# Three of seven skip products moved into the states' accumulation, and an instruction planner that chooses by replays

## The chip, the cores and the metric

The kernel runs on one core of one Trainium2 chip. The metric is the device time of one launch in microseconds (us), median of three runs. The engines are named as in the profile: PE is TensorE's matmul side and PEld its weight loads, DVE is VectorE, ACT is ScalarE, POOL is GpSimd, SP is the engine that issues nearly all DMAs.

## The reference

Four residual layers on x of shape (4, 1024, 256), all in float32. Layer 1 is causal attention, layers 2 and 4 are the same channel mix, layer 3 is a state-space layer. The change lies in layer 3.

```python
xn = layernorm(x) * ln_g + ln_b
x_proj, z = split(xn @ W_in.T + b_in)              # 256 columns each
z = silu(z)
B_proj = x_proj @ W_B.T * dt.mean()                # 16 states
x_mean = causal_conv(B_proj, A_mean)               # along the tokens, per state
y = (x_mean @ W_C.T + D_skip * x_proj) * z
x = x + y @ W_out.T + b_out

# layers 2 and 4 (the mix)
r = sigmoid(xr @ W_r.T); k = relu(xk @ W_k.T) ** 2 # xr, xk: x mixed with the token before
x = x + r * (k @ W_v.T)
```

## The kernel before

**Tiling.** Each of the four batches b is two halves j = 2b and 2b + 1 of 512 tokens. A half is kept once by rows (128 tokens x 256 features, four times) and once turned, as columns: two blocks c of 128 features x 512 tokens. A product of one 128 x 128 weight block with 512 columns is the unit of work here. Two PSUM pools hold products: four single banks ("bank") and two double banks ("pair").

**Seven products instead of eight.** For a batch the 2 x 2 weight blocks meet a 2 x 2 arrangement of data (two feature blocks, two halves). `seven_products` (L821) makes the four results with seven products rather than eight, in the manner of Strassen and Winograd: `weight_sums` gives four sums of weight blocks, `stream_sums` (L796) gives four sums T1 to T4 of data blocks, on POOL or DVE. Each product p1 to p7 goes to a bank of its own, and VectorE adds it to what is there. This is used for the attention's queries (tiles p_qs), for the gates z (p_zs), for the skip D_skip * x_proj (p_ss, written to the tiles skip) and for the last mix's keys (p_gks).

**The states' share.** The convolution gives x_mean; SP writes it to memory (m_dram) and reads it back turned (xmT), per batch with four DMAs each way (`states_in`, L1829). For batch 0 `skip(0)` and `skip(1)` make the skip by plain products into a pair, and `mix_states` (L1920) adds x_mean @ W_C.T in the same banks. For batches 1 to 3 `skips_of_batch` (L1866) makes the skip with seven products, and `mix_states_apart` (L1880) makes x_mean @ W_C.T into the two pairs, as four matmuls of 16 rows that lie in four different row groups of TensorE. Then `grown` (L1899) adds these to the skip on VectorE, and `gated` (L1903) multiplies by z on POOL or DVE. `state_outputs` multiplies by W_out (tiles pr_pyo), and x is grown by the result (L1956).

**Order by hand, order by plan.** The order of TensorE's work is written out by hand in the kernel's main part. Gates and skips of batches 1 to 3 form one stream, `all_gates`, and `more_gates(n)` takes n products from it between other units, to cover the time in which those wait. The orders of the other engines come from `Order`: all work is logged with estimated costs and needs, `_due` (backwards) gives each operation the time by which TensorE needs it, and `_run` plays the program forwards on a model and takes, engine by engine, what is due first. `finish` (L178) tries 20 plans (share, margin, wait) in five rounds each; after a round, `_hurry` brings forward the dues of what TensorE waited for. The plan and dues with the earliest modelled end are then played once more, and this time the instructions are emitted. The same plan rules the whole program.

Of the kernel before, what the change touches and what calls it, by code (L numbers as in the profile page):

```python
# [4 lines left out]

# [39 lines left out]
def columns(n, k=1):  # L45

    return 2 * k * max(n * 0.845e-3, 0.105)
# [5 lines left out]
class Order:  # L53
# [23 lines left out]
        for share, margin in ((0.2, 2.5), (0.1, 1.5), (0.3, 4.0), (0.2, 1.5), (0.1, 2.5))  # L77
        for wait in (0.0, 0.08, 0.15, 0.22)
    ]
    ROUNDS = 5  # L80
    TRIALS = 4
    BANKS = {"bank": 4, "pair": 2}
# [95 lines left out]
    def finish(self):  # L178
        dues = self._due()
        self.made = {e["key"]: n for n, e in enumerate(self.log) if e["key"] is not None}  # L180
        self.ends = []
        best = math.inf
        for plan in self.PLANS:
            self.due = list(dues)
            for k in range(self.ROUNDS):
                used = list(self.due)
                end = self._run(plan, False)
                self.ends.append((end, k, plan))
                if end < best:
                    best, chosen = end, (plan, used)  # L190
                for key, wait in self.waits:
                    self._hurry(key, wait)
        plan, self.due = chosen
        self._run(plan, True)

    def _hurry(self, key, wait):

# [8 lines left out]
    def _run(self, plan, emits):  # L206
        self.SHARE, self.MARGIN, self.WAIT = plan
        self.emits = emits
        self.waits = []
        self.now = self.at = 0.0  # L210
        self.free, self.ready, self.offered = {}, {}, []
        self.queue = self.port = 0.0
        self.waiting = {}
        self.psum = {kind: [0.0] * k for kind, k in self.BANKS.items()}
        for n, e in enumerate(self.log):
            if e["kind"] == "op":
                self._enter(n)
            elif e["kind"] == "known":
                self._done(e["key"], e["time"])
            elif e["kind"] == "take":  # L220
                heapq.heappop(self.psum[e["takes"]])
            else:
                self._unit(e)
        while self.offered:
            self._step()
        return max(self.now, *self.free.values())
# [57 lines left out]
    def _step(self):  # L284
        self.at, k = self._first()
        time, n = self.offered.pop(k)
        e = self.log[n]
        end, _, engine, emit = self._way(time, n)
        engine, _, port = engine.partition("+")
        self.free[engine] = end  # L290
        if port or engine == "POOL":
            self.port = end
        if self.emits:
            emit()
        if e["frees"]:
            heapq.heappush(self.psum[e["frees"]], end + self.LAG)
        if e["moves"]:
            for k, work in enumerate(e["moves"]):
                issued = end - (len(e["moves"]) - 1 - k) * self.log[n]["cost"] / len(e["moves"])
                self.queue = max(self.queue, issued + self.FLIGHT) + work  # L300
            self._done(e["key"], self.queue + self.LANDING)
        else:
            self._done(e["key"], end + e["lag"])
# [46 lines left out]
def hybrid_kernel(  # L350
# [470 lines left out]
    def seven_products(key, sums_key, a, s_of, src, t_of, out, bias, needs, there):  # L821


        u = lazy(lambda: slot(f"u_{key}")[:, :HALF])

        def unit(r, w, data, need):
            p = lazy(lambda: bank(f"p{r}_{key}"))
            o.unit(
                f"{key}.p{r}", columns(HALF), needs + need,
                lambda: nc.tensor.matmul(p(), lhsT=w(), rhs=data(), start=True, stop=True), "bank",  # L830
            )
            return p

        def add(name, r, p, more, dst, e, need, last=True):

            def emit():
                if e is None or bias is None:
                    nc.vector.tensor_add(dst(), p(), more())
                else:
                    nc.vector.scalar_tensor_tensor(  # L840
                        dst(), p(), bias(e), more(), ALU.add, ALU.add
                    )
            o.op(
                f"{key}.{name}", [f"{key}.p{r}"] + [f"{key}.{k}" for k in need],
                ("DVE", dve(HALF) + 0.03, emit), frees="bank" if last else None,
            )

        def block(e, h):
            return lambda: out(e, h)

        p = unit(1, lambda: a(0, 0), lambda: src(0)[:, 0, :], there)
        o.op(f"{key}.u1", [f"{key}.p1"], *copies(u, p), frees="bank")
        yield
        p = unit(2, lambda: a(0, 1), lambda: src(0)[:, 1, :], there)
# [12 lines left out]
        add("c22", 5, p, u, block(1, 1), 1, ["u3"], last=False)  # L867
        add("v12", 5, p, block(0, 1), block(0, 1), 0, ["u3"])
        yield
        p = unit(3, lambda: s_of(4), lambda: src(1)[:, 1, :], there)  # L870
        add("c12", 3, p, block(0, 1), block(0, 1), None, ["v12"])
        yield
# [993 lines left out]
    def skips_of_batch(b):  # L1866

        there = columns_of(2 * b) + columns_of(2 * b + 1)
        src = lambda h, xb=(xnT[2 * b], xnT[2 * b + 1]): xb[h]()
        for j in (2 * b, 2 * b + 1):  # L1870
            skips[j] = lazy(lambda j=j: cols(f"skip_{j}"))
        sb = [skips[2 * b], skips[2 * b + 1]]
        sums_of_batch(b + 1)
        yield from seven_products(
            f"ss{b}", f"zs{b}", wx_block, lambda k: x_sums[:, k - 1, :], src, sums_of_batch(b),
            lambda e, h: sb[h]()[:, e, :], lambda e: b_skip[:, e : e + 1],
            ["x_sums", "b_all"], there,
        )

    def mix_states_apart(b):  # L1880

        for h in range(2):
            py[2 * b + h] = lazy(lambda h=h: pair(f"py_{2 * b + h}"))

        def emit():
            for e in range(KC):
                for h in range(2):
                    k = 2 * e + h
                    nc.tensor.matmul(
                        py[2 * b + h]()[:, ts(e, HALF)],  # L1890
                        lhsT=w_c[k * GRP : k * GRP + S, ts(e, P)],
                        rhs=xmT[b]()[k * GRP : k * GRP + S, ts(h, HALF)],
                        start=True,
                        stop=True,
                    )

        def grown(j, e):
            t = skips[j]()[:, e, :]
            nc.vector.tensor_add(t, py[j]()[:, ts(e, HALF)], t)  # L1899

        def gated(engine, j, e):
            t = z[j]()[:, e, :]
            engine.tensor_mul(t, t, skips[j]()[:, e, :])  # L1903

        o.unit(f"pm{b}", 1.0, ["w_c", f"xmT{b}"], emit, "pair", many=2)
        for h in range(2):
            j = 2 * b + h
            for e in range(KC):
                o.op(
                    f"g{e}.{j}", [f"pm{b}", f"ss{b}.c{e + 1}{h + 1}"],  # L1910
                    ("DVE", dve(HALF) + 0.03, partial(grown, j, e)),
                    frees="pair" if e else None,
                )
                o.op(
                    f"y{e}.{j}", [f"g{e}.{j}", f"z{e}.{j}"],
                    ("POOL", 1.05, partial(gated, nc.gpsimd, j, e)),
                    ("DVE+port", dve(HALF), partial(gated, nc.vector, j, e)),
                )
# [208 lines left out]
    for b in range(NB):  # L2127
        states_in(b)
    skip(1)
    more_gates(8)  # L2130
    mix_states(0)
    more_gates(8)
    outputs(0)
    more_gates(5)
    mix_states_apart(1)
    outputs(1)
    more_gates(4)
    outputs(2)
    more_gates(4)
    mix_states_apart(2)  # L2140
    outputs(3)
    more_gates(3)
# [86 lines left out]
```

## Time and profile before

| what | us |
|---|---|
| median of 3 runs | 465.42 (465.42 to 465.47) |
| profiled execution | 465.0 |
| its span, first to last instruction | 463.1 |
| PE busy in the span | 456.0 |
| DVE busy | 390.2 |
| ACT busy | 220.8 |
| POOL busy | 143.1 |

The profile is of one execution, so a sum made from it is made against its own 465.0 and its span of 463.1. The median of the runs shown is 0.4 above that execution. The program's stages follow each other in the span roughly so: loads and first scores to 20; attention with the first mix between its rows to 287; the states' convolution to 310; skips, gates and outputs of the state layer to 385, the last mix's first halves among them; the rest of the last mix to the end. Matmuls overlap a little in the records, so their cost is better read from start to start than from the listed duration.

### The profile page before, as it was taken

What the parts mean: (1) busy time and instruction counts of PE and PEld (TensorE: products, weight loads), DVE (VectorE), ACT (ScalarE), POOL (GpSimd) and SP (SyncE); (2) the same over time, 40 slices, a digit from 0 to 9 for tenths busy, and PEclk for the clock granted to TensorE, in tenths of its full rate; (3) what the DMA queues carried; (4) which work ended last, traced back from release to release, by engine and by line L of the source; (5) the groups of instructions that cost most, each with busy time, mean ns of one, the idle gap of its engine ahead of it and who ended that gap; (6) DMA issues with size and microseconds to landing.
All of it is one profiled execution on the core that took longest, in us unless ns stands there. A gap on an engine that the chain in (4) does not pass through costs nothing.

```text
span 463.1 us, 6634 instructions
## 1 busy us (share of the span) xinstructions
PE 456.0 (98%) x2052; PEld 312.5 (67%) x2052; DVE 390.2 (84%) x931; ACT 220.8 (48%) x463; POOL 143.1 (31%) x149
## 2 busy tenths in 40 slices
PE   8999999999999999999999999999999999999996
PEld 5766785667786667786777775474565758675875
DVE  3687769899969999889999977459889999999962
ACT  3422414454342433333556567441458777664652
POOL 3000102112013213121271354962052616826340
PEclk9999999999999999999999999999999999999999
DMA  8047876848455763427866989603022024252442
GB/s 242 21 127 203 250 190 168 222 132 258 117 135 139 221 194 93 118 62 237 224 177 182 275 268 271 260 17 88 11 92 91 1 86 144 81 147 99 129 144 84
DMA packets 84915, 69.44 MB, mean 150 GB/s; under 512 B 20160, under 2 KB 82576, under 8 KB 84880
## 3 DMA queue, kind: packets, MB, share of 16 engines
q1 hardware_dynamic: 84064, 68.76, 50.8%
q10 hardware_dynamic: 816, 0.26, 0.2%
q8 instruction: 16, 0.26, 0.2%
q14 instruction: 19, 0.16, 0.1%
HBM read 40.54 MB, written 28.45 MB: 149 GB/s over the span
## 4 chain that ended last, share of the span: by engine, by line
PE 86%; DVE 8%; issue 2%; DMA 1%; POOL 1%; ACT 1%; SPq 0%; DVEq 0%; POOLq 0%
PE po L1597 13%; PE sc L1492 13%; PE pv L1464 5%; PE p_zs L830 4%; PE p_ss L830 4%; PE p_qs L830 2%; PE p_gks L830 2%; PE py L1848 2%; PE pc L1798 2%; PE dust L1282 1%; DMA blocks_a<-rows_a 1%; PE pr_g0.pr L881 1%; PE pb L1735 1%; PE pp_a0.pq L774 1%; PE pr_g0.pv L881 1%
## 5 line engine op out<-in xcount | busy, mean ns | idle before, releaser
L1597 PE MATMUL po<-v,prT 128*128 128x256 f32 x288 | 67.7, 380 | 0.1
L1492 PE MATMUL sc<-xa,q 128*128 128x512 f32 (+3 forms) x192 | 67.0, 486 | 0.0
L1597 PEld LDWEIGHTS po<-v,prT 128*128 128x128 f32 x288 | 54.2, 189 | 11.6 <-issue 2.6
L1513 ACT ACTIVATE pr<-pr,nmx 128x128 f32<-128x128 f32 (+7 forms) x32 | 24.7, 773 | 64.6 <-DVE pr L1508 57.7
L1492 PEld LDWEIGHTS sc<-xa,q 128*128 128x128 f32 x192 | 35.1, 190 | 24.5 <-issue 19.6
L1464 PE MATMUL pv<-wv,xa 128*128 128x257 f32 x128 | 32.9, 380 | 0.0
L642 POOL TENSOR_TENSOR rs_a<-ve_a,minus_half 128x4 f32<-128x4 f32 x7 | 7.1, 1010 | 76.8 <-DVE ve_a L629 76.8
L1044 POOL TENSOR_TENSOR x<-x,r_f 128x512 f32<-128x512 f32 x16 | 20.3, 1271 | 33.0 <-DVE r_f L1038 32.5
L642 POOL TENSOR_TENSOR rs_h<-ve_h,minus_half 128x8 f32<-128x8 f32 x8 | 13.2, 1647 | 52.5 <-DVE ve_h L631 52.5
L1464 PEld LDWEIGHTS pv<-wv,xa 128*128 128x128 f32 x128 | 23.6, 191 | 7.8 <-issue 3.6
L1508 DVE TENSOR_SCALAR_CACHE_REDUCE pr<-sc,v 128x128 f32<-128x128 f32 (+7 forms) x32 | 26.2, 818 | 1.1
L1550 DVE STREAM_TRANSPOSE prT<-pblocks 128x384 f32<-128x384 f32 (+7 forms) x30 | 23.8, 793 | 2.4 <-DMA pblocks<-exps 2.3
L642 POOL TENSOR_TENSOR rs_f<-ve_f,minus_half 128x4 f32<-128x4 f32 x8 | 8.4, 1053 | 47.1 <-DVE ve_f L629 28.8
L1044 POOL TENSOR_TENSOR x<-x,r_g 128x512 f32<-128x512 f32 x14 | 18.9, 1371 | 11.0 <-DVE r_g L1038 11.0
L1641 POOL TENSOR_TENSOR x<-x,bout_r 128x512 f32<-128x512 f32 x16 | 20.0, 1279 | 4.5 <-ACT x L1634 4.5
L1606 DVE SCALAR_TENSOR_TENSOR x<-po,rsm,x 128x256 f32<-128x256 f32 x32 | 15.0, 470 | 4.3 <-PE po L1597 3.8
L1474 DVE TENSOR_TENSOR v<-pv,bv_r 128x257 f32<-128x257 f32 x32 | 13.4, 418 | 5.6 <-PE pv L1464 5.6
L930 DVE SCALAR_TENSOR_TENSOR xr_g<-hT_g,mur,xr_g 128x512 f32<-128x512 f32 x16 | 17.3, 1112 | 0.0
L663 ACT ACTIVATE xn_f<-x,mrs_f,rs_f 128x256 f32<-128x256 f32 x18 | 9.8, 592 | 15.5 <-DVE mrs_f L651 15.5
L1634 ACT ACTIVATE x<-x,mrs_h,rs 128x256 f32<-128x256 f32 x32 | 16.9, 592 | 0.0
L1903 POOL TENSOR_TENSOR z<-z,skip 128x512 f32<-128x512 f32 x9 | 13.1, 1462 | 10.9 <-DVE skip L1899 10.7
L663 ACT ACTIVATE xn_g<-x,mrs_g,rs_g 128x256 f32<-128x256 f32 x23 | 12.4, 589 | 8.3 <-DVE mrs_g L626 6.7
(458 smaller groups left out, 1089.8 us busy)
## 6 DMA issues: line engine op xcount, KB each, us to landing
hk<-r_dram SPq DMA_DIRECT2D x16, 512.0 KB, 9.2
rows_g<-xn_g SPq DMA_DIRECT2D x8, 512.0 KB, 2.9
blocks_g<-rows_g SPq DMA_DIRECT2D x32, 128.0 KB, 2.8
x<-in_L_attn_a_X_dram SPq DMA_DIRECT2D x7, 512.0 KB, 4.9
rows_f<-xn_f SPq DMA_DIRECT2D x7, 512.0 KB, 3.0
blocks_f<-rows_f SPq DMA_DIRECT2D x28, 128.0 KB, 2.7
rows_h<-xn_h SPq DMA_DIRECT2D x7, 512.0 KB, 3.7
blocks_h<-rows_h SPq DMA_DIRECT2D x28, 128.0 KB, 3.2
```

Of the source, the lines that this page charges most:

```text
L642: nc.gpsimd.tensor_tensor(rs()[:, :k].rearrange("p k n -> p (k n)"), ve()[:, :k].rearrange("p k n -> p (k n)"), minus_half[:, : k * NH], A ...
L663: nc.scalar.activation(place(n), split(row(n)), AF.Identity, bias=mrs()[:, k - 1, n : n + 1], scale=rs()[:, k - 1, n : n + 1],)
L830: lambda: nc.tensor.matmul(p(), lhsT=w(), rhs=data(), start=True, stop=True), "bank",
L930: nc.vector.scalar_tensor_tensor(t()[:, c, :], hT()[:, c, :HALF], mu1[:, c : c + 1], t()[:, c, :], ALU.mult, ALU.add,)
L1044: nc.gpsimd.tensor_add(xg, xg, r()[:, ts(g, 2), :])
L1464: nc.tensor.matmul(pv()[:, : D + 1], lhsT=xaj()[:, c, ts(n, P)], rhs=wv[:, c, :], start=(c == 0), stop=(c == KC - 1),)
L1492: nc.tensor.matmul(sc()[:, k * HALF : k * HALF + w], lhsT=qh()[:, c, ts(n, P)], rhs=keys[k]()[:, c, :w], start=(c == 0), stop=(c == KC - 1),)
L1508: nc.vector.tensor_scalar(dst, src, v[2 * b + h]()[:, n, D : D + 1], None, ALU.add, ALU.min, accum_out=nmx(),)
L1513: nc.scalar.activation(p()[:, :nk], p()[:, :nk], AF.Exp, bias=nmx(), scale=-1.0, accum_out=sm())
L1550: nc.vector.transpose(dst()[:, : NH * width].rearrange("p (k m a) -> p k m a", m=NH, a=GRP), blocks().rearrange("p m (k a) -> p k m a", a= ...
L1597: nc.tensor.matmul(po()[:, :D], lhsT=src()[:, ts(n, P)], rhs=v[2 * b + n // NH]()[:, n % NH, :D], start=(n == 0), stop=(n == t),)
L1641: nc.gpsimd.tensor_add(xg, xg, bout_r.unsqueeze(1).to_broadcast([P, 2, D]))
```

## The change

It has two parts.

First, the skips. The products p2, p4 and p3 of the seven each go into one result only, and nothing else is made from them. After the change they are no longer evicted on their own. `skips_of_batch` makes only p1, p6, p7 and p5 and keeps the partial sums u1, u4, u3, u5 in the four blocks of the skip tiles. `mix_states_apart` makes the other three with start=True and stop=False in the pairs' banks and lets the 16-row matmuls of the states accumulate onto them; the fourth bank, k == 3, is opened by the states' matmul itself. `grown` adds the bias b_skip along with the partial sum. The stream `all_gates` becomes nine turns shorter, and the numbers of `more_gates` are changed with it.

Second, the choice of a plan. After each modelled run, `_replays` plays the order that it gave six times more, with costs stretched at random (DVE up to 3%, ACT 4%, POOL 25%) and landings of transfers up to 0.6 us late, the seeds being fixed. The mean end of these replays, not the end of the run, is what plans are compared by, and the waits that occur in them are what `_hurry` is given.

```diff
@@ class Order @@
+    SAMPLES = 6
+    SPREAD = {"DVE": 0.03, "ACT": 0.04, "POOL": 0.25}
+    LATE = 0.6
@@ finish @@
                 used = list(self.due)
-                end = self._run(plan, False)
+                self._run(plan, False)
+                end = self._replays()
...
+    def _replays(self):
+        lost, ends = {}, 0.0
+        for k in range(self.SAMPLES):
+            rng = random.Random(k)
+            ends += self._replay(rng, lost)
+        self.waits = [(key, t / self.SAMPLES) for key, t in lost.items() if t > 0.1 * self.SAMPLES]
+        return ends / self.SAMPLES
...
+    def _replay(self, rng, lost):
+        for n, way in self.trail:
...
+            at = max(at, free.get(engine, 0.0), port if shared or engine == "POOL" else 0.0)
+            spread = self.SPREAD.get(engine, 0.0)
+            at += cost * (1.0 + spread * rng.random())
...
+                at = queue + self.LANDING + self.LATE * rng.random()
@@ skips_of_batch @@
-        yield from seven_products(
-            f"ss{b}", f"zs{b}", wx_block, lambda k: x_sums[:, k - 1, :], src, sums_of_batch(b),
-            lambda e, h: sb[h]()[:, e, :], lambda e: b_skip[:, e : e + 1],
-            ["x_sums", "b_all"], there,
-        )
+        u1, u2, u3, u5 = block(0, 0), block(0, 1), block(1, 0), block(1, 1)
+        p = unit(1, lambda: wx_block(0, 0), lambda: xnT[2 * b]()[:, 0, :], there)
+        o.op(f"{key}.u1", [f"{key}.p1"], *copies(u1, p), frees="bank")
+        yield
+        p = unit(6, lambda: x_sums[:, 1, :], lambda: T(2), [f"zs{b}.T2"])
+        add("u2", 6, p, u1, u2, "u1")
+        yield
+        p = unit(7, lambda: x_sums[:, 2, :], lambda: T(3), [f"zs{b}.T3"])
+        add("u3", 7, p, u2, u3, "u2")
+        yield
+        p = unit(5, lambda: x_sums[:, 0, :], lambda: T(1), [f"zs{b}.T1"])
+        add("u5", 5, p, u3, u5, "u3", last=False)
+        add("u4", 5, p, u2, u2, "u3")
+        yield
@@ mix_states_apart @@
         def emit():
+            for h, e, w, data in (
+                (0, 0, wx_block(0, 1), xnT[2 * b]()[:, 1, :]),
+                (0, 1, wx_block(1, 1), T(4)),
+                (1, 0, x_sums[:, 3, :], xnT[2 * b + 1]()[:, 1, :]),
+            ):
+                nc.tensor.matmul(
+                    py[2 * b + h]()[:, ts(e, HALF)], lhsT=w, rhs=data, start=True, stop=False
+                )
...
-                        start=True,
+                        start=(k == 3),
...
-            nc.vector.tensor_add(t, py[j]()[:, ts(e, HALF)], t)
+            nc.vector.scalar_tensor_tensor(
+                t, py[j]()[:, ts(e, HALF)], b_skip[:, e : e + 1], t, ALU.add, ALU.add
+            )
...
-        o.unit(f"pm{b}", 1.0, ["w_c", f"xmT{b}"], emit, "pair", many=2)
+        o.unit(
+            f"pm{b}", columns(HALF, 3) + 1.05,
+            ["w_c", "x_sums", "b_all", f"xmT{b}", f"zs{b}.T4"] + there, emit, "pair", many=2,
+        )
@@ main part @@
     skip(1)
-    more_gates(8)
+    more_gates(6)
     mix_states(0)
-    more_gates(8)
+    more_gates(5)
     outputs(0)
-    more_gates(5)
+    more_gates(3)
     mix_states_apart(1)
     outputs(1)
-    more_gates(4)
+    more_gates(3)
     outputs(2)
-    more_gates(4)
+    more_gates(3)
     mix_states_apart(2)
```

More of the change, by code (lines that the diff above doesn't have):

```diff
@@ L2 @@
 import math
+import random
 from contextlib import ExitStack
@@ L194, in finish @@
         self._run(plan, True)
+    def _replays(self):
[6 more added lines that the diff above has]
+    def _replay(self, rng, lost):
+        now = queue = port = 0.0
+        free, ready = {}, {}
+        psum = {kind: [0.0] * k for kind, k in self.BANKS.items()}
+        for n, way in self.trail:
+            e = self.log[n]
+            if e["kind"] == "known":
+                ready[e["key"]] = e["time"]
+                continue
+            if e["kind"] == "take":
+                heapq.heappop(psum[e["takes"]])
+                continue
+            last, at = None, 0.0
+            for k in e["needs"]:
+                if ready[k] > at:
+                    last, at = k, ready[k]
+            if e["kind"] == "unit":
+                for _ in range(e["many"] if e["takes"] else 0):
+                    at = max(at, heapq.heappop(psum[e["takes"]]))
+                if last is not None and at > now + 0.1:
+                    lost[last] = lost.get(last, 0.0) + at - now
+                now = max(now, at) + e["cost"]
+                ready[e["key"]] = now + self.LAG
+                continue
+            engine, shared, cost = way
+            if e["moves"]:
+                at = max(at, queue - self.FLIGHT - 0.5)
+            at = max(at, free.get(engine, 0.0), port if shared or engine == "POOL" else 0.0)
+            spread = self.SPREAD.get(engine, 0.0)
+            at += cost * (1.0 + spread * rng.random())
+            free[engine] = at
+            if shared or engine == "POOL":
+                port = at
+            if e["frees"]:
+                heapq.heappush(psum[e["frees"]], at + self.LAG)
+            if e["moves"]:
+                for k, work in enumerate(e["moves"]):
+                    issued = at - (len(e["moves"]) - 1 - k) * e["cost"] / len(e["moves"])
+                    queue = max(queue, issued + self.FLIGHT) + work
+                at = queue + self.LANDING + self.LATE * rng.random()
+            else:
+                at += e["lag"]
+            if e["key"] is not None:
+                ready[e["key"]] = at
+        return max(now, *free.values())
     def _hurry(self, key, wait):
@@ L208, in _run @@
         self.emits = emits
-        self.waits = []
+        self.waits, self.trail = [], []
         self.now = self.at = 0.0
@@ L218, in _run @@
             elif e["kind"] == "known":
+                self.trail.append((n, None))
                 self._done(e["key"], e["time"])
             elif e["kind"] == "take":
+                self.trail.append((n, None))
                 heapq.heappop(self.psum[e["takes"]])
@@ L223, in _run @@
                 self._unit(e)
+                self.trail.append((n, None))
         while self.offered:
@@ L287, in _step @@
         e = self.log[n]
-        end, _, engine, emit = self._way(time, n)
+        end, start, engine, emit = self._way(time, n)
         engine, _, port = engine.partition("+")
+        self.trail.append((n, (engine, port, end - start)))
         self.free[engine] = end
@@ L1868, in skips_of_batch, with block, unit, add @@
         there = columns_of(2 * b) + columns_of(2 * b + 1)
-        src = lambda h, xb=(xnT[2 * b], xnT[2 * b + 1]): xb[h]()
+        key = f"ss{b}"
+        T = sums_of_batch(b)
         for j in (2 * b, 2 * b + 1):
             skips[j] = lazy(lambda j=j: cols(f"skip_{j}"))
-        sb = [skips[2 * b], skips[2 * b + 1]]
         sums_of_batch(b + 1)
-        yield from seven_products(
-            f"ss{b}", f"zs{b}", wx_block, lambda k: x_sums[:, k - 1, :], src, sums_of_batch(b),
-            lambda e, h: sb[h]()[:, e, :], lambda e: b_skip[:, e : e + 1],
-            ["x_sums", "b_all"], there,
-        )
+        def block(e, h):
+            return lambda: skips[2 * b + h]()[:, e, :]
+        def unit(r, w, data, need):
+            p = lazy(lambda: bank(f"p{r}_{key}"))
+            o.unit(
+                f"{key}.p{r}", columns(HALF), ["x_sums", "b_all"] + need,
+                lambda: nc.tensor.matmul(p(), lhsT=w(), rhs=data(), start=True, stop=True), "bank",
+            )
+            return p
+        def add(name, r, p, more, to, need, last=True):
+            o.op(
+                f"{key}.{name}", [f"{key}.p{r}", f"{key}.{need}"],
+                ("DVE", dve(HALF) + 0.03, lambda: nc.vector.tensor_add(to(), p(), more())),
+                frees="bank" if last else None,
+            )
[13 more added lines that the diff above has]
+        yield
     def mix_states_apart(b):
@@ L1883, in mix_states_apart @@
             py[2 * b + h] = lazy(lambda h=h: pair(f"py_{2 * b + h}"))
+        T = sums_of_batch(b)
         def emit():
+            for h, e, w, data in (
[6 more added lines that the diff above has]
+                )
             for e in range(KC):
@@ L1898, in grown @@
             t = skips[j]()[:, e, :]
-            nc.vector.tensor_add(t, py[j]()[:, ts(e, HALF)], t)
+            nc.vector.scalar_tensor_tensor(
+                t, py[j]()[:, ts(e, HALF)], b_skip[:, e : e + 1], t, ALU.add, ALU.add
+            )
         def gated(engine, j, e):
@@ L1903, in gated @@
             engine.tensor_mul(t, t, skips[j]()[:, e, :])
-        o.unit(f"pm{b}", 1.0, ["w_c", f"xmT{b}"], emit, "pair", many=2)
+        there = columns_of(2 * b) + columns_of(2 * b + 1)
+        o.unit(
+            f"pm{b}", columns(HALF, 3) + 1.05,
+            ["w_c", "x_sums", "b_all", f"xmT{b}", f"zs{b}.T4"] + there, emit, "pair", many=2,
+        )
         for h in range(2):
@@ L1909, in mix_states_apart @@
                 o.op(
-                    f"g{e}.{j}", [f"pm{b}", f"ss{b}.c{e + 1}{h + 1}"],
+                    f"g{e}.{j}", [f"pm{b}", f"ss{b}." + (("u1", "u4"), ("u3", "u5"))[e][h]]
+                    + ([f"ss{b}.u2"] if (e, h) == (0, 0) else [])
+                    + ([f"ss{b}.u5"] if (e, h) == (1, 0) else []),
                     ("DVE", dve(HALF) + 0.03, partial(grown, j, e)),
```

## The prediction

> **What bounds the kernel now.** First the page's head and busy rows, then the busy times by stage.
>
> ```profile
> span 463.1 us, 6634 instructions
> PE 456.0 (98%) x2052; PEld 312.5 (67%) x2052; DVE 390.2 (84%) x931; ACT 220.8 (48%) x463; POOL 143.1 (31%) x149
> ```
>
> ```profile
> core 0: us, PE busy (x) PEld busy (x) DVE busy (x) ACT busy (x) POOL busy (x), PEclk, DMA share, GB/s
> 0.00:20.00 20.00, 18.49 (x78) 11.90 (x79) 10.20 (x41) 7.64 (x16) 4.75 (x18) 1.00 0.51 151
> 20.00:287.00 267.00, 266.82 (x1095) 188.05 (x1094) 236.14 (x652) 114.18 (x216) 60.93 (x60) 1.00 0.65 182
> ...
> 310.00:320.00 10.00, 10.00 (x24) 4.09 (x22) 9.76 (x10) 0.58 (x1) 6.02 (x4) 1.00 0.28 77
> 320.00:350.00 30.00, 30.00 (x105) 17.36 (x105) 25.68 (x42) 14.84 (x48) 6.74 (x8) 1.00 0.18 54
> 350.00:385.00 35.00, 34.97 (x136) 22.72 (x135) 33.54 (x57) 27.93 (x85) 13.40 (x16) 1.00 0.24 76
> 385.00:426.00 41.00, 39.33 (x159) 29.49 (x157) 39.52 (x65) 24.24 (x44) 25.07 (x23) 1.00 0.32 98
> ```
>
> TensorE (PE) is the bound: 0.18 us idle in 267 us of attention and first mix, none in 310 to 350. Only its work, or its few late waits, can give time back. From 350 on VectorE (DVE) is 96% busy, and there TensorE begins to wait: 1.67 us in 385 to 426. The timeline of TensorE shows the waits, in the last column:
>
> ```profile
> 358.44 3.72 PE L881 MATMUL pr_g0.pr<-w_r,xr_g 128*128 128x256 f32 x16
> 362.17 1.99 PE L881 MATMUL pr_pyo0.4_3308<-w_out,z 128*128 128x256 f32 x8
> ...
> 395.68 1.99 PE L881 MATMUL pr_g2.pr<-w_r,xr_g 128*128 128x256 f32 x8 [0.69 <-ACT r_g L1016]
> ...
> 425.48 1.10 PE L830 MATMUL p_gks<-T_gks,w_fk 128*128 128x512 f32 x2 [0.98 <-DVE u_gks L765]
> ```
>
> Counted from start to start, the loss is larger than the brackets, since the first matmul after a wait runs 0.1 us longer. Eight matmuls of L881 take 1.73 from start to start (1.89 listed), so the half from 393.10 should have ended at 394.83, and the next starts at 395.68: 0.85, with the slow restart 0.95. The half p_gks from 422.62 should end at 424.34, and 425.48 follows: with its restart 1.2. The row of 358.44 takes 3.73 to the next start where its sisters take 3.45, and begins 0.18 late; 362.17 restarts 0.1 slow; one p_gks at 376 loses 0.25. That is 0.8 for the three, and 2.95, say 3.0, for all. This is all that the change can win where it acts.
>
> **The change, TensorE.** Before, a batch b of 1 to 3 has seven skip products (p_ss, 0.86 each from start to start) and a states' unit of four K=16 matmuls in four row groups, 1.07 together. After, four products stay and three open the states' banks: 4 + 3, and the same 1.07. So 0 us of matmuls is saved. The change between full and row-grouped matmuls costs about 0.1 at either side (336.02 and 337.09 in the timeline), once per batch before and after.
>
> **VectorE.** Rows of 310 to 385, by form:
>
> ```profile
> L840 DVE SCALAR_TENSOR_TENSOR skip<-p_ss,b_skip,u_ss 128x512 f32<-128x512 f32 x9 | 6.7, 744 | 0.5 <-issue 0.2 <-PE p_ss L830 0.2
> L1899 DVE TENSOR_TENSOR skip<-py,skip 128x512 f32<-128x512 f32 x10 | 6.6, 681 | 1.0 <-PE py L1889 1.0
> L838 DVE TENSOR_TENSOR skip<-p_ss,skip 128x512 f32<-128x512 f32 x3 | 2.1, 692 | 0.2
> L838 DVE TENSOR_TENSOR u_ss<-p_ss,skip 128x512 f32<-128x512 f32 x3 | 2.1, 686 | 0.3 <-PE p_ss L830 0.2
> ```
>
> Back to back such adds follow at 0.60 and the three-operand ones at 0.66. Per batch before: c11, c21, c22, v12 with the bias (4 x 0.66), u2, u3, c12 plain (3 x 0.60), four grown adds (4 x 0.60): 6.84. After: u2, u3, u5, u4 plain (2.40), four grown with the bias (2.64): 5.04. Saved 1.8 per batch, 5.4 in all. The first copy, u1, stays. The Trainium skill (VectorE: DVE Perf Modes, the errata-adjusted table and the measured formula under it) gives a tensor_tensor of N elements (N+151)/0.96 ns, 0.69 us alone, and no surcharge for a scalar operand; by it nine instructions gone save 6.2. I take the trace: durations overlap, and bias adds are 0.06 dearer.
>
> The saving itself lies beside TensorE's work. It counts only where DVE is late. The wait before 358.44 is put down by the trace to the L840 add of 357.65 (skip), one of those removed. Before 395.68 the four banks are held: the adds of the pyo0.6 and pyo1.6 outputs run at 394.26 and 396.32 although their products ended near 391.4 and 393.1, and r_g's second add runs at 393.66, in a VectorE queue without a gap. By the unit of batch 3 (381.6) that queue has 5.4 us less to do. So I let the 0.8 and the 0.95 go whole. Before 425.48 it is VectorE's 1.24 and 1.51 us instructions (mrs_g, xn_g at 422 to 424, beside long GpSimd instructions); half of 1.2 goes. Gain: 0.8 + 0.95 + 0.6 = 2.35.
>
> **What moves.** With fewer turns taken at each call, outputs come earlier in TensorE's order: 11 products instead of 16 stand ahead of the outputs of half 0. Two new waits follow. First, the states of batch 0. SP's rows:
>
> ```profile
> 310.12 2.27 SPq L1817 DMA_DIRECT2D m_dram<-xm  x4
> 313.85 8.37 SPq L1834 DMA_DIRECT2D xmT<-m_dram  x13
> ```
>
> The fourth transfer of batch 0 is issued at 315.83, and the tile's view gives 2.5 to 2.8 us from issue to landing (median 2.7): 318.35 to 318.65. Before, eight products cover it (unit at 320.14). After, six: 313.18 + 6 x 0.86 = 318.33, with the switch 318.43. So 0 to 0.3 late, with the slow restart up to 0.4; I take 0.3. The skill (DMA: Bandwidth & Descriptors, Anatomy of one DMA) fits a fixed cost near 2.0 us, on GpSimd's path; by it the landing is 318.0 and the wait 0. The row is of this very transfer, so it decides. While this unit waits, everything behind it on TensorE waits; no SP or GpSimd instruction is moved past it.
>
> Second, the outputs of half 0 start at about 324.2 instead of 328.2. From 313.2 VectorE must do before them 3.4 of T_zs, 2.4 of skips, some 4.0 of gates, 1.3 of y: 11.1 in 11.0 us. It is just enough when the last evictions are put behind; bounds 0 and 0.6, taken 0.2. From there on its use is as before. By the outputs of half 2 it was, from 313.2 to 344.1, T_zs 3.4, three sets of seven adds 13.3, y 2.6, output adds 2.4, grown 2.4 and some 4 of the next mix and gates: 28.1 in 30.9 us. After, 13.3 becomes 9.2 and grown 2.6, and they come 4 us earlier: 24.2 in 26.9. The states' unit now needs both pairs of banks for 3.65 instead of 1.07 us; the pairs were free 6 us early at 336, so nothing. T4 and x^T live longer by up to 8 us; nothing in the trace waits for their room.
>
> **The new way to choose.** The chosen plan sets every engine's order, in the attention too, which the edit of the skips never touches. TensorE loses 0.18 us in 20 to 287: another order can hardly win there, it can only lose. Nothing in the trace prices a changed order; bounds are -0.5 (two small losses near 92 and 181 go) and +5 (five waits like 395.68's). By the nearest row, such a wait is 0.95; plans judged under late GpSimd and transfers should leave few, so half a wait, 0.4, is taken.
>
> **Sum.** -2.35 + 0.3 + 0.2 + 0.4 = -1.45 on a span of 463.1, in an execution of 465.0; the median of the runs shown is 465.42. Forecast: 464.0.
>
> **Rivals.** (1) The late waits belong to the last mix's own order (GpSimd's rs_g and x, bank turns), not to VectorE's backlog: 358.44's 0.5 alone is won, new waits of 0.5 to 1 eat it: 465.4. For it: ACT's r_g of pr_g2.pr sits idle until the product ended, and POOL instructions of 1.3 to 2 us stand in the chain at 393 to 398. Against: the chain before them is VectorE from 386. (2) Slower: the new order stalls TensorE in the attention, where each block of turned exponents passes SP, memory and VectorE before po (L1597). Each such wait is 0.95 by the nearest row. Two cost 1.9 + 0.5 - 2.35 = 0, three 2.85 + 0.5 - 2.35 = 1.0: from three on the kernel is slower. Three to five give 466.4 to 468.3, four 467.4. For it: no slack at all in 267 us of TensorE. Against: replays punish exactly these. (3) The same plan wins again and nothing moves outside the states' stage: -1.85, 463.6, within my case.
>
> **How the numbers follow.** Forecast's case 0.50, from 462.4 (all 3.0 won, nothing new) to 464.5; rival 1 0.17, 464.5 to 466.4; rival 2 0.33, 466.4 to 468.3, the fewer waits the likelier. Some 0.2% (0.93 us) is what a measurement here tells from no change. Faster 0.51, same 0.16, slower 0.33. The range that leaves out 2 in 10 goes from 462.5 to 467.3; the likeliest case alone is 462.4 to 464.5.
>
> **What would show it.** Right: TensorE's busy time stays within 0.5 us of 456.0; L838, L840 and L1899's successors fall by nine; the waits at 358, 395 are gone; idle in the last mix falls to under 1 us. The step at the states of batch 0 shows as a gap before the first K=16 unit near 318.5. Wrong: a bracketed wait of TensorE between 20 and 287, above all before po or sc; or idle in 385 to 426 still at 1.7 with VectorE less than 90% busy.

## The result: 1.2% slower, and the profile after

The changed kernel takes 470.3 us (median; 470.15 to 470.99), the kernel before on the same chip 465.42: a ratio of 1.0116 (95% interval 1.0101 to 1.0131), 4.9 us more, where 464.0 was forecast. The profile shows a span of 468.6, 5.4 above the 463.1 of before. The head and busy rows of the page after:

```profile
span 468.6 us, 6639 instructions
PE 456.4 (97%) x2052; PEld 312.8 (67%) x2052; DVE 388.5 (83%) x935; ACT 215.8 (46%) x454; POOL 138.0 (29%) x146
```

TensorE does the same 2052 matmuls in the same busy time (456.0 before), so the loss is time in which it stood or ran slowly. VectorE's part is not what was forecast: 935 instructions where before had 931, and 388.5 us busy against 390.2. A plan also chooses which engine takes an operation, and this one gave VectorE other work for the nine instructions that the skips' part takes from it (ScalarE has 454 where it had 463, GpSimd 146 where it had 149). The busy times by stage, in the stretches that were shown of before:

```profile
core 0: us, PE busy (x) PEld busy (x) DVE busy (x) ACT busy (x) POOL busy (x), PEclk, DMA share, GB/s
...
20.00:287.00 267.00, 263.06 (x1080) 186.28 (x1079) 236.13 (x640) 109.20 (x209) 64.23 (x63) 0.99 0.61 176
...
320.00:350.00 30.00, 30.00 (x105) 17.20 (x104) 25.74 (x43) 13.47 (x46) 7.81 (x9) 1.00 0.23 68
350.00:385.00 35.00, 34.33 (x125) 22.22 (x124) 32.24 (x57) 26.10 (x76) 11.14 (x14) 1.00 0.21 67
385.00:426.00 41.00, 40.17 (x169) 30.19 (x168) 38.32 (x66) 23.84 (x46) 19.42 (x18) 1.00 0.32 99
```

In 20 to 287, where 0.18 us was idle, 3.9 now are, and the clock column is no longer 1.00. That is ahead of every operation that the skips' part edits. TensorE's waits by what they are for, and its timeline at the longest:

```profile
PE pt_f7.hT L821 <- DVE xn_f L722: 3.3, 1, 3.3
PE p_gks L895 <- DVE x L2066: 0.8, 1, 0.8
PE p_gks L895 <- DVE u_gks L830: 0.7, 1, 0.7
PE pr_g0.pr L946 <- ACT skip L829: 0.7, 1, 0.7
PE p_qs L895 <- DVE xa L796: 0.5, 1, 0.5
```

```profile
258.25 1.88 PE L839 MATMUL pp_f6.pk<-xk_f,w_fk 128*128 128x512 f32 x4
263.44 1.40 PE L821 MATMUL pt_f7.hT<-ident,xn_f 128*128 128x128 f32 x8 [3.31 <-DVE xn_f L722]
264.63 3.31 PE L839 MATMUL pp_f6.pk<-xk_f,w_fk 128*128 128x512 f32 x4
```

pt_f7.hT (the turn of the last attention row block for the first mix) waits 3.31; from start to start 3.47 are lost. The four matmuls pp_f6.pk behind it take 3.31, where the four of 258.25 took 1.88. The granted clock says why:

```profile
20.00:259.00 239.00, 238.38 (x989) 168.91 (x988) 213.89 (x584) 96.51 (x188) 47.67 (x49) 1.00 0.61 172
259.50:263.40 3.90, 0.63 (x2) 0.00 (x0) 3.20 (x9) 1.59 (x3) 2.38 (x3) 1.00 0.84 252
263.40:267.60 4.20, 4.16 (x12) 2.53 (x13) 4.10 (x11) 1.50 (x3) 3.21 (x3) 0.59 0.99 316
```

A mean of 0.59 over 4.2 us stands for some 1.7 us lost. Taken between the starts of the same TensorE instructions, the 5.4 us of span are: 3.9 up to pt_f7.hT, 1.6 from there to pt_h7 (such a turn for the state layer's last half), 0.5 in the middle of the last mix (pr_g0.pv to pr_g5.pr), and -0.6 from an earlier first product. From the states' convolution to pr_g0.pv, the stage of the moved products, it is 80.25 us after and 80.13 before: nothing won, nothing lost.

**What made xn_f late.** VectorE from 249, then GpSimd:

```profile
249.48 1.27 DVE L716 SCALAR_TENSOR_TENSOR mrs_h<-rs_h,mv_h 128x4 f32<-128x4 f32 x2
250.68 2.65 DVE L722 TENSOR_SCALAR xn_h<-x,mv_h,rs_h 128x256 f32<-128x256 f32 x2
253.25 0.15 DVE L1675 RECIPROCAL rsm<-sm 128x1 f32<-128x1 f32 x1
253.32 1.72 DVE L722 TENSOR_SCALAR xn_h<-x,mv_h,rs_h 128x256 f32<-128x256 f32 x2
...
259.06 0.44 DVE L1671 SCALAR_TENSOR_TENSOR x<-po,rsm,x 128x256 f32<-128x256 f32 x1
```

```profile
249.39 5.18 POOL L1706 TENSOR_TENSOR x<-x,bout_r 128x512 f32<-128x512 f32 x4 [5.34 <-ACT x L1699]
```

and the same work on VectorE before, where GpSimd was idle beside it:

```profile
249.80 0.22 DVE L651 SCALAR_TENSOR_TENSOR mrs_h<-rs_h,mv_h 128x4 f32<-128x4 f32 x2
249.94 1.05 DVE L657 TENSOR_SCALAR xn_h<-x,mv_h,rs_h 128x256 f32<-128x256 f32 x3
```

Two mrs_h and four xn_h, some 1.6 us of work where GpSimd is idle, lasted from 249.48 to 255.04. In the trace each of the four GpSimd adds (1.27 to 1.32 each) has one VectorE instruction beside it that ends 0.02 to 0.16 after it: one mrs_h took 1195 ns instead of 150, three xn_h 1361 to 1398 instead of 402. The add x <- po (L1671), the last attention row, stands behind them in VectorE's queue and ran at 259.06 where it ran at 255.22 before; its statistics, rs_f and xn_f follow, and pt_f7.hT waits. The Trainium skill (SBUF — State Buffer, Who interferes with whom) has the two engines share one pair of ports, which a tensor_scalar in its two-port mode holds for its whole length. The xn_h rows, all tensor_scalar, agree with such a block; mrs_h, another kind of instruction with two inputs in SBUF, was held as long.

### The profile page after: what moved, and what is told of

Its sections match the earlier page's. It is cut to its first block, busy times and chain, and to the rows that moved or that the text cites. A ratio compares the mean times of both kernels' runs of the same rounds, so it can differ in the third digit from the quotient of the medians.

```text
span 468.6 us, 6639 instructions
## 1 busy us (share of the span) xinstructions
PE 456.4 (97%) x2052; PEld 312.8 (67%) x2052; DVE 388.5 (83%) x935; ACT 215.8 (46%) x454; POOL 138.0 (29%) x146
## 4 chain that ended last, share of the span: by engine, by line
PE 72%; DVE 12%; DMA 8%; SPq 3%; issue 2%; ACT 1%; POOL 0%; DVEq 0%; POOLq 0%
PE sc L1557 10%; PE po L1662 10%; PE pv L1529 5%; PE p_zs L895 4%; PE p_ss L1947 2%; PE p_gks L895 2%; PE py L1985 2%; SPq L790 2%; PE py L1913 2%; DMA exps<-pr 2%; PE pc L1863 2%; DVE xk_g L995 1%; DMA rows_f<-xn_f 1%; PE p_qs L895 1%; DMA pblocks<-exps 1%
## 5 line engine op out<-in xcount | busy, mean ns | idle before, releaser
L1671 DVE SCALAR_TENSOR_TENSOR x<-po,rsm,x 128x256 f32<-128x256 f32 x32 | 15.1, 471 | 3.8 <-PE po L1662 3.4
L992 ACT ACTIVATE xk_f<-hT_f,muk 128x512 f32<-128x512 f32 x16 | 11.1, 717 | 11.7 <-DVE hT_f L796 10.2
L668 DVE BATCH_NORM_STATS2 st_a<-x 128x6 f32<-128x256 f32 x32 | 13.0, 406 | 2.8 <-DMA x<-in_L_attn_a_X_dram 2.8
L995 DVE SCALAR_TENSOR_TENSOR xr_g<-hT_g,mur,xr_g 128x512 f32<-128x512 f32 x16 | 13.5, 872 | 1.3 <-ACT xr_g L992 1.3
```

The costliest lines, as they stand in the source:

```text
L995: nc.vector.scalar_tensor_tensor(t()[:, c, :], hT()[:, c, :HALF], mu1[:, c : c + 1], t()[:, c, :], ALU.mult, ALU.add,)
```

## The experiments

Theory A: the newly chosen order of the other engines costs, the skips' part itself does not. Rival B: the skips' part costs. An order here is each engine's queue and the choice of the engine for an operation. All times are medians beside runs of the kernel before on the same chip (464.35 to 464.89 there; ratios against those).

**1. One part alone, twice.**

```diff
 # skip_only: the skips' part, plans judged as before
-                self._run(plan, False)
-                end = self._replays()
+                end = self._run(plan, False)
 # replay_only: skips and more_gates as before, plans judged by replays
```

> The skips' part alone; plans are chosen by the end of the modelled run, as before. Theory A (the loss of 4.9 us is one wait of 3.5 us before the turned rows of half 7, with 1.6 us of slower TensorE clock behind it, and comes with the order that the replays chose): this kernel has no such wait at 260 us, keeps a clock of 1.00 and takes 463.5 to 466. Rival B (the shorter stream of skips brings the loss, whatever chooses the plan): 468 to 471.

> The replays alone, with the skips of before. Theory A in its strong form (replays choose orders that are bad on the chip): 467 to 471, with a wait of TensorE over 1 us before 310 us. Its weak form (the replays are as good as the run's end, and the changed kernel drew a bad order by chance): 464.5 to 467. Rival B: within 1 us of 465.4.

skip_only took 468.73 (ratio 1.0083, 1.0068 to 1.0098), replay_only 466.37 (1.0037, 1.0023 to 1.0051). Each part alone makes the kernel slower. But their waits lie at different places: skip_only has none at 260 but 1.4 before pt_h7 and about 5.7 in the last mix (start to start; 3.0 before), at a clock of 0.999; replay_only has 2.45 at 160 in the attention. skip_only's number pointed to B, and replay_only's fits the weak form of A. Yet in both a new order had been chosen, since a changed log gives another plan: the parts were not separated from the order.

**2. The wait at 260.** pool_late moves GpSimd's four adds out of the way; dust_in_wait fills the wait with products of which nothing is used.

```diff
 # pool_late, the changed kernel's order with one move on GpSimd
+        self._moved(trail, ["h0.o0", "h0.o1", "h1.o0", "h1.o1"], "f5.x1")
 # dust_in_wait, behind the products of f6.pk0
+                for _ in range(15):
+                    nc.tensor.matmul(dust, lhsT=idle[:, :P], rhs=idle, start=True, stop=True)
```

> The changed kernel in its own chosen order, with four GpSimd adds of the state layer (x + bout_r for halves 0 and 1) moved behind f5's second add on GpSimd; every other engine keeps its order to the instruction. Theory A1 (these four adds, back to back from 249.4 to 254.6, hold a port that VectorE's mrs_h and xn_h need; VectorE spends 5.5 us there on some 1.7 us of work, and is 3.8 us late at the last row of the attention): VectorE's five instructions take under 2.5 us, the wait before pt_f7 falls under 0.5 us, the clock stays at 1.00, and the time is 465 to 466. Rival A2 (VectorE is late by its own order, two pairs of turned state columns ahead of the last row's add): the wait stays above 2 us and the time above 468.

> The changed kernel with 15 idle bf16 matmuls (3.2 us) behind f6's first key product, that is inside the wait of 3.5 us; all other engines keep their order. Theory A3 (the slow matmuls of 263 to 267 us, 0.85 instead of 0.43 us each, follow from TensorE's idle time): they run at 0.43 us, the wait itself stays, and the time falls by 1.4 to 1.6 us, to 468.7 to 468.9. Rival (the clock was lowered for another reason): no change, 470.3.

pool_late took 469.76 (1.0106, 1.0072 to 1.0139), not the 465 to 466 expected. The wait at 260 is gone (pt_f7.hT starts at 259.83), and VectorE takes mrs_h in 0.22 and xn_h at 0.40 each, 1.57 us in all: GpSimd's adds were the cause of that wait. But the profile has this instead:

```profile
PE pt_h7.T L847 <- DVE xn_h L748: 3.3, 1, 3.3
```

In their new place the four adds stand in a row of six on GpSimd, and VectorE was held beside them again. GpSimd and VectorE in pool_late, then the same VectorE instructions before:

```profile
261.85 8.76 POOL L1732 TENSOR_TENSOR x<-x,bout_r 128x512 f32<-128x512 f32 x6
263.35 3.24 DVE L1021 SCALAR_TENSOR_TENSOR xk_f<-hT_f,muk,xk_f 128x512 f32<-128x512 f32 x2
```

```profile
262.65 1.38 DVE L930 SCALAR_TENSOR_TENSOR xk_f<-hT_f,muk,xk_f 128x512 f32<-128x512 f32 x2
```

With the two xr_f behind them (1.75 and 1.72 instead of 0.72 each) that is 6.7 us instead of 2.8. VectorE stays late up to the last half of the state layer (ve_h at 286.62, 283.83 before), whose xn_h pt_h7 waits for. So moving the adds shows what held TensorE at 260, and the price moved on with them. Whether this order would be free of a wait with the adds where VectorE has no such work was not tried.

dust_in_wait took 468.88 (1.009, 1.0075 to 1.0105), 1.2 us less than the changed kernel in ratio, as expected. The wait stays, only the clock is kept:

```profile
260.39 3.40 PE L846 MATMUL dust<-idle 128*128 128x512 bf16 x14
263.83 1.07 PE L821 MATMUL pt_f7.hT<-ident,xn_f 128*128 128x128 f32 x8
264.74 1.91 PE L839 MATMUL pp_f6.pk<-xk_f,w_fk 128*128 128x512 f32 x4
```

The four matmuls take 1.91 again, so the slow ones followed from the idle time. Some 1.2 to 1.6 of the 5.4 were the clock.

**3. The skips' part with nothing chosen anew, and other choices with nothing changed.** skips_old_order makes every engine follow the order of before, written down; the moved operations are left out or take their partner's place. old_second and old_third are the kernel before, unchanged, but emitted by the plans that it ranks second and third; new_second is the changed kernel by the plan that its replays rank second.

```diff
 # skips_old_order: finish follows a list instead of choosing
+ORDER = """wq_n1/ACT ... ss3.u5/DVE ... none22/DVE"""
 # old_second (old_third: (0.2, 1.5, 0.22), k == 3; new_second: (0.1, 2.5, 0.15), k == 3)
-                if end < best:
+                if plan == (0.1, 1.5, 0.22) and k == 2:
```

> The skips' part of the change alone, with every engine made to follow the order of the kernel before: the three open products moved into the states' units, c11, c21 and c12 gone, the bias in the grown adds. Nothing is chosen anew. Theory A (the skips' part is harmless, and the loss of the changed kernel is the newly drawn order alone): 464.0 to 465.3 against about 464.8 for the kernel before on the same chip, no wait of TensorE between 20 and 300. If VectorE's relief of 5.4 us also wins late waits, as the prediction had it, 462.4 to 463.8. Theory B (the skips' part itself costs: the states' unit holds TensorE or banks longer, or comes too late): 467 to 470, with a wait in 310 to 350.

> The kernel before, its operations untouched, but emitted in the order of the second of its own plans (share 0.1, margin 1.5, wait 0.22, third round of hurrying) instead of the first. Theory A (any newly drawn order costs, because the order of the kernel before is a lucky one of many): 466 to 470, with one or two waits of TensorE at places where the kernel before has none. Rival (orders of near plans are equally good, and the loss is due to the changed operations or to the replays): 464.3 to 465.8.

> As before, with the order of the third plan (share 0.2, margin 1.5, wait 0.22, fourth round). Theory A: 466 to 471, with new waits at other places than the second plan's. Rival: 464.3 to 466.

> The changed kernel, with the order of the plan that its replays put second (share 0.1, margin 2.5, wait 0.15) instead of first. Theory A (the replays do not see the wait at 260, so their ranking says little of the chip and the times of their plans scatter): anywhere from 465.5 to 472, as likely below 470.3 as above, with waits at other places. Rival (the replays rank plans rightly and the loss is in the operations): over 470.3, by about 1 us.

| kernel | median us | ratio to before | 95% interval |
|---|---|---|---|
| skips_old_order | 465.58 | 1.0027 | 1.0017 to 1.0036 |
| old_second | 476.18 | 1.0257 | 1.0231 to 1.0282 |
| old_third | 472.33 | 1.018 | 1.0157 to 1.0203 |
| new_second | 469.87 | 1.0116 | 1.0095 to 1.0136 |

This decides it. The unchanged kernel loses 11.8 us by its own second plan and 8.0 by its third, more than was expected of either, with TensorE's 2052 matmuls in the same order in all of them. What differs is the other engines' queues and which of them takes an operation (VectorE has 944 and 933 instructions there, 931 before). TensorE's waits in old_second, with the length of each in all, the number and the longest:

```profile
PE p_gks L830 <- DVE T_gks L813: 2.8, 2, 1.6
PE pt_h7.T L756 <- DVE xn_h L657: 2.6, 3, 1.3
PE pt_f7.hT L756 <- DVE xn_f L657: 1.6, 1, 1.6
PE pp_g6.pk L774 <- DVE xk_g L930: 1.5, 1, 1.5
PE p_gks L830 <- DVE x L1956: 0.9, 1, 0.9
```

The same two places, pt_f7 and pt_h7, appear among them. The order of before was the best of the draws seen here. Its planner had ranked it first, but the slowest of the three second, so the ranking is a weak guide, and any edit of the log draws again. The replays did not mend that: new_second has the same time as their first choice. Of the changed kernel's 1.16%, the skips' part with the order held accounts for 0.27 (1.2 us; the time lies just above the 464.0 to 465.3 expected) and the order for the other 0.9 (about 4.1 us). That split is not pure: skips_old_order also has other numbers of products in more_gates (6, 6, 3, 4, 4, 2, 1, where the changed kernel has 6, 5, 3, 3, 3, 3, 3), so TensorE's own order differs a little behind 310. The 3.9 and 1.6 at the wait at 260 lie ahead of that.

**4. Where VectorE's relief went.** The skips' part with the old order has exactly nine VectorE instructions fewer (922 against 931) and 6.4 us less busy time (383.8 against 390.2) (a relief that the changed kernel with its own plan does not show), and is still not faster. TensorE's waits from 20 on in skips_old_order:

```profile
PE p_gks L1076 <- DVE u_gks L1011: 1.0, 1, 1.0
PE pr_g2.pr L1127 <- ACT r_g L1262: 0.7, 1, 0.7
PE pr_pyo0.4_3290 L1127 <- ACT r_g L1262: 0.6, 1, 0.6
PE p_qs L1076 <- DVE xa L977: 0.2, 1, 0.2
```

The two largest of before are there in their old size: 0.85 before pr_g2.pr's second half (0.85 before), 1.14 in p_gks (1.15 before), start to start. VectorE at the states of batch 3, before and in skips_old_order, shows why:

```profile
381.43 0.74 DVE L840 SCALAR_TENSOR_TENSOR skip<-p_ss,b_skip,u_ss 128x512 f32<-128x512 f32 x1
382.81 1.29 DVE L1899 TENSOR_TENSOR skip<-py,skip 128x512 f32<-128x512 f32 x2 [0.64 <-PE py L1889]
```

```profile
380.01 0.69 DVE L2135 TENSOR_TENSOR skip<-p_ss,skip 128x512 f32<-128x512 f32 x1
383.45 0.75 DVE L2182 SCALAR_TENSOR_TENSOR skip<-py,b_skip,skip 128x512 f32<-128x512 f32 x1 [2.75 <-PE py L2172]
```

VectorE is done earlier, then stands 2.75 us instead of 0.64 for py, the states' product of batch 3, and everything behind it in its queue follows from TensorE's time, as before. The time saved ahead of this point ends here.

Then the waits themselves were attacked. Five instructions moved in the old order (old_mended, and with the skips' part skips_mended), then three more, two of them the transposes hT_g of group 2 moved into the gap of 2.75 (skips_cashed, old_cashed).

```diff
 # old_mended, skips_mended: moves in the list
+ g0.g0 before g1.xkm1 (ACT); on DVE: g3.mrs after gks0.v12, g1.rv1 before g3.hT0,
+ gks2.u1 before g6.mrs, g6.xn0 after gks2.c11
 # old_cashed, skips_cashed: the same, and on DVE
+ s4.x0 before g0.5; g2.hT1 and g2.hT0 before g1.6
```

> The kernel before with five instructions moved in its own order, nothing else: ScalarE's copy g0.g0 ahead of xk_g; VectorE's mrs of group 3 behind v12; r_g's second add of g1 ahead of a transpose, so that the second half of pr_g2.pr takes that bank and no longer the first half's; u_gks of the third keys ahead of mrs_g and xn_g. If the late waits belong to the order of single instructions (who stands ahead of whom), those at 395.68 (0.95) and 425.48 (1.2) go and the time falls by 2.0 to 2.7: 461.7 to 462.4 against about 464.4 for the kernel before on the same chip. If they belong to VectorE's backlog (the forecast's reading), they come back a few us later and the time falls by less than 1.

> The skips' part in the order of before (the kernel that took 465.58), with the same five moves. Its late waits were 0.87 at 361.6, 0.36 at 377.7, 0.95 at 396.3 and 1.2 at 426.3. By the reading of single instructions all four go: 3.0 to 3.5 us less than 465.58, that is 462.1 to 462.6, no better than the kernel before with the same moves, since VectorE's relief is worth nothing where TensorE sets the pace. By the backlog reading the relief adds to it: 1 us or more below the kernel before with the same moves.

> skips_mended (464.69), with two more moves on VectorE: the add of output pyo0.4 ahead of a states' add, so that the second product of the first keys no longer waits 0.94 for the copy of the first; and the two transposes hT_g of group 2 ahead of the states' adds of batch 3, into the 3.1 us in which VectorE stands idle before them, since there it waits for TensorE's states. In 383 to 408 VectorE is busy 24.1 of 25 us; if that stage is VectorE's, and the relief of the skips' part is lost only because VectorE waits in order at the states, then up to 1.3 us of work now leaves the stage: waits at 402 and 407 (1.5 together) shrink by about 0.9, the 0.94 at 365 goes, and the time is 462.6 to 463.3. If the relief can't be cashed, only the 0.94 goes: 463.5 to 464.1, and if something else comes back, 464.3 or more.

> The same seven moves in the kernel before, without the skips' part. There VectorE stands idle only 0.64 before the states' adds of batch 3, so the transposes moved ahead find at most that: the 0.94 at 367 goes and waits of 1.3 at 402 and 407 shrink by at most 0.6: 463.4 to 464.2 against about 464.6 for the kernel before. The difference to skips_cashed is what the relief of VectorE is worth: 0.3 to 1.0 by the reading above, 0 if it is lost anyway.

(The expectations count the moves as five and seven; three were added, so eight.) Results: old_mended 464.85 (0.9996, 0.9988 to 1.0005), skips_mended 464.69 (0.9991, 0.9979 to 1.0003), skips_cashed 464.70 (0.9993, 0.9986 to 1.0001), old_cashed 464.54 (0.9992, 0.9984 to 1.0001). All four cannot be told from the kernel before, the skips' part makes no difference between them, and all four lie above the times at which the moves would have paid. The aimed waits at 396 and 425 did go, and others came. skips_mended:

```profile
PE pr_g3.pr L1127 <- DVE u_gks L1084: 0.8, 1, 0.8
PE p_gks L1076 <- ACT u_gks L1010: 0.7, 1, 0.7
PE p_gks L1076 <- DVE T_gks L1059: 0.3, 1, 0.3
```

skips_cashed:

```profile
PE pr_g3.pr L1127 <- DVE u_gks L1084: 0.8, 1, 0.8
PE p_gks L1076 <- DVE T_gks L1059: 0.7, 1, 0.7
PE pr_g1.pr L1127 <- DVE ka_g L1084: 0.6, 1, 0.6
```

In old_mended the two waits gone are worth 2.15; new ones of 0.94 at 366, 0.36 at 402 and 0.95 more at 407 take back 2.25. My reading by single instructions fell, and so did the one by cashing the gap. In skips_cashed the transposes do run in the gap, at 381.82 instead of 383.86, after a wait of 2.63 for their own transfer; but VectorE then waits 0.85 for pr_g0.pv and its queue is ahead by only 0.26 at 387, which is what TensorE itself is ahead by there. What fits all four: from the states of batch 3 to 408 VectorE is busy 24.0 of 25 us before and 24.1 in skips_mended, on work that the change does not touch. A wait mended inside this stretch comes back at its end. That VectorE's work there alone sets it was not tried by taking some of it away; it stays a reading.

No version here beats the kernel before by more than can be measured.

## Why the prediction was wrong, step by step

The forecast of 464.0 rested on two terms that failed. The 2.35 us of won waits came to nothing, since VectorE's next entry needed the product of the very unit by which it should have been ahead; and the new order, put at 0.4, cost about 4.1. The mechanism of the first was wrong, the size of the second. Term by term:

- **TensorE, 0 us of matmuls:** right; 456.4 busy, with the same count.
- **VectorE saves 5.4 us:** right with the order held, and the size low: nine instructions fewer, and 6.4 us less busy. In the changed kernel the new plan took most of that back (four instructions more than before, 1.7 us less). It did not matter for the time.
- **2.35 of late waits won:** wrong, 0 won. With the order held the losses after 350 were 3.9 (0.87 at 361, 0.26 at 375, 0.36 at 377, 0.95 at 396, 0.26 at 407, 1.22 at 426) against 3.0. The step that failed is "By the unit of batch 3 (381.6) that queue has 5.4 us less to do. So I let the 0.8 and the 0.95 go whole." The queue had less to do, but its next entry needs the product of that very unit, and VectorE stood 2.75 us for it instead of 0.64. I had also read the wait before 395.68 as four banks held by late VectorE adds. The bracket said "<-ACT r_g", ScalarE's copy of the first half of pr_g2.pr: it ended at 395.63, and the second half started at 395.68. My reading now is that the second half was given the bank of its first half, and another one once r_g's second add was moved earlier, since the wait went (old_mended). No bank is on record, so this is not shown. The 0.8 at 358 changed into 0.87 at 361, behind ScalarE's xk_g.
- **States of batch 0, +0.3, and outputs of half 0, +0.2:** both 0. From the convolution to the states' unit it is 15.90 us in the changed kernel and 15.91 with the old order: two products of 0.86 less than the 17.63 of before, and no wait.
- **The new order, +0.4, bounds -0.5 to +5:** this term decided. It measured about 4.1 for the chosen plan (one wait of 3.5 before pt_f7.hT and 1.6 of clock behind it), and 11.8 and 8.0 for two other plans of the unchanged kernel, beyond my upper bound. I took half of a wait of 0.95 because "plans judged under late GpSimd and transfers should leave few". That was wrong: the replays chose the plan with the wait of 3.5. Why they missed it is a reading of their code, not a result: they play each order with GpSimd and VectorE sharing the port in the order of the plan, while on the chip the adds started when their input came (the bracket "5.34 <-ACT x" at 249.39), beside mrs_h and xn_h.
- **Rival 2** had the occasion and the stage, a stall of TensorE in the attention at a new order. It had neither the path (turned exponents before po; it came through GpSimd's adds, VectorE and xn_f) nor the price: not three to five waits of 0.95 but one of 3.5 that also cost 1.6 of clock. Its 466.4 to 468.3 ended below the 470.3 measured.
- **Rival 1**, that the late waits belong to the last mix's own order, is nearer to what the old order showed than the forecast's case: it took 465.58 where the rival said 465.4, and new waits took back what went. That the chosen plan would cost more was not in it.

## What to carry to other kernels

Where a planner sets every queue of a kernel that is full to 98%, an edit is not tested until its order is held: emit the edited kernel in the old order first, and run the second-best plan of the old kernel to learn what a draw of the order costs (here 8.0 and 11.8 us, more than any term of the change). Instructions taken from a queue help only up to the next entry that waits for the bound engine; look for that entry before counting the gain. And a wait seen in the trace should be followed to the releaser that its bracket names: here it was right, and my story about late VectorE adds was not.

## What the runs showed of the hardware

The granted clock fell behind some waits of TensorE and not behind others, and the length of the wait does not decide it alone. After 3.5 us lost it fell in all four runs of the changed kernel (0.996 in each). After pool_late's wait of 3.31 before pt_h7 two of four runs show 0.993, and these take 471.1 and 471.4 where the other two take 468.3 and 468.5. Behind the gap of 2.45 at 160 in replay_only the profiled run shows 0.62 for the next 4.5 us and 0.995 as a whole; its other four runs show 0.998 to 1.0. In old_second a wait of 1.61 was enough, with an onset some 1.2 us after TensorE had started again; the slow matmuls lost another 1.6:

```profile
261.50:262.70 1.20, 1.20 (x8) 0.90 (x9) 1.20 (x4) 0.29 (x1) 0.00 (x0) 1.00 0.78 253
```

```profile
262.70:265.20 2.50, 2.50 (x6) 0.95 (x5) 2.47 (x6) 1.29 (x2) 1.27 (x1) 0.53 1.00 246
```

A wait of 1.61 at 429.5 in new_second left it at 1.00, and so did a longer one in old_third, 3.11 in the last mix:

```profile
429.56 1.96 PE L830 MATMUL p_gks<-T_gks,fk_sums 128*128 128x512 f32 x4 [3.11 <-DVE T_gks L813]
```

```profile
429.60:434.00 4.40, 4.40 (x11) 2.01 (x12) 4.30 (x9) 1.83 (x4) 0.00 (x0) 1.00 0.29 105
```

The waits of up to 1.15 in the kernel before cost no clock (1.00 in the rows, 1.0 as a whole). The Trainium skill (TensorE: Matmul & The Clock Gate, Why this matters for your kernels) warns of gaps above about 3 us; here waits of 1.61 and 2.45 did it too, one of 3.11 did not, and the measurement decides. What else it takes was not tried and stays open. Where the clock did fall behind pt_f7.hT, it cost about as much again as the wait in old_second (1.6 behind 1.61) and about half in the changed kernel (1.6 behind 3.5).
